# Late query features from a quarter of the array's rows per head, and reciprocals spread by a product with ones

## The chip, the cores and the metric

One core of a Trainium2 chip runs a whole decoder layer in one launch. The metric is the device time in microseconds (us). The kernel before took 2324.54 us, the median of three runs (2317.61 to 2330.41).

The engines of the core have the names of the profile: PE is the matrix engine (PEld its loading of the stationary operand), DVE, ACT and POOL are the vector, scalar and GpSimd engines, SP is the engine from whose queue most DMAs are issued. SBUF is the working memory with 128 partitions, PSUM the memory that PE writes, in banks of 128 x 512 fp32.

## The reference

A pre-norm decoder layer on x of 2 x 2048 tokens by 512: `x + attn(ln(x))`, then cross attention on a context of 154 tokens, then a mixture of experts. Only the first part is touched, a linear attention with 16 heads of 32 dimensions and 128 features:

```python
q_proj = _elu1(jnp.einsum('bhnd,hdf->bhnf', q, proj_matrix))
k_proj = _elu1(jnp.einsum('bhnd,hdf->bhnf', k, proj_matrix))
kv = jnp.einsum('bhnf,bhnd->bhfd', k_proj, v)
attn = jnp.einsum('bhnf,bhfd->bhnd', q_proj, kv)
k_sum = k_proj.sum(axis=2)
z = 1.0 / (jnp.einsum('bhnf,bhf->bhn', q_proj, k_sum) + 1e-08)
attn = attn * z[..., None]
out = attn.transpose(0, 2, 1, 3).reshape(b, n, d)
return out @ w_out + b_out
```

`_elu1(x)` is x + 1 for x > 0 and exp(x) otherwise. All is fp32.

## The kernel before

**Blocks and chunks.** The 4096 tokens are 8 blocks of 512 (`TB`), 4 to each batch (`bpb`). Everything is held with features in the partitions and tokens in the free dimension. A chunk is a pair (block b, c) with c from 0 to 3: 128 of the 512 dimensions, that is 4 heads of 32.

**Products in parts.** Where fp32 accuracy is wanted from the `fp32r` format, an operand is kept as a high part (an ACT copy) and a low part (`low`, line 116: source minus high part), and a product is three terms, high x high, low x high and high x low (`TERMS`, line 142; `product`, line 144).

**Queries and keys for the features.** A head has only 32 rows. `to_heads` (line 356) stores a chunk's projection, high and low, in DRAM (`qd`). `stack` (line 292) loads it back as 96 rows: high, low, high, in three DMAs. The projection matrix lies as 96 rows too (`pst`: high, high, low), so that one product of 96 rows gives the sum of all three terms. `query_features` (line 476) makes one such product for one head, into one of the 4 PSUM banks of the pool `sc`, and `features` (line 361) makes `_elu1` of it: two ACT passes and one DVE instruction.

**Sums.** `numerators` (line 485) multiplies the four heads' features with `kv`, each head in its own quarter of the array's columns; `denominators` (line 507) does the same with the key sums into a bank `pd` that is held for the block's four chunks. `columns.matmul` (line 229) keeps these in program order.

**Reciprocals.** `reciprocals` (line 522) adds the epsilon, stores the 16 x 512 denominators in DRAM (`dd`), loads them as 128 x 64 (`turned`), takes the reciprocal on DVE and stores it (`stored`, `zd`). `load_reciprocals` (line 548) loads them for two chunks, each head's row broadcast to that head's 32 partitions, in four DMAs into a tile `zr`.

**Attention's end.** `attended` (line 558) multiplies numerators by `zr` on POOL, copies to the high part on ACT and takes the low part on DVE. `attention_out` (line 567) multiplies by `w_out` and adds x and the bias (`out_tile`, line 304). For the first batch the numerators lie in DRAM meanwhile (`numd`), and `load_numerators` (line 544) fetches 1 MB for a block through POOL's queue.

**Order.** `Dense` (line 175) holds a list of generators of large products; `dense.fill(n)` issues n of them, and `dense.after(n, do)` does something n products later. Three loops matter:

- The key loop (line 1306) goes over all 8 blocks, with the first batch's queries made during the second batch's keys, one head at a time. At its item (7, 3, 0) it loads what the next stage wants first (line 1320).
- A short loop (line 1334) ends those queries.
- The late loop (line 1346) makes the second batch's queries, 16 chunks in 17 steps. A step issues two heads' features, 13 products of `dense` (14 from step 12), a quarter of an attended block, and the same again; then the sums of the chunk before. `ahead` (line 1345) says which block's halves are attended in which step. Queries are loaded a step ahead, reciprocals likewise.

Behind the late loop the cross attention begins (line 1390); the last block is attended in its first steps.

**Buffers.** `big` has 17 buffers of 8 KB per partition (`eight`), `work` the tiles of `half` (9) and of `pair_of` (4), `ps` and `sc` four PSUM banks each. A framework places the waits and orders the instructions of each engine, except where program order is kept.

Of the kernel before, what the change touches and what calls it, by code (L numbers as in the profile page):

```python
# [17 lines left out]
P = 128  # L18
# [12 lines left out]
Z_EPS = 1e-8  # L31
LAG = 3
SC = 4
GROUP = 2


@with_exitstack
def decoder_layer(
# [65 lines left out]
    def pair_of(name, n=TB):  # L104
        return work.tile([P, 2, n], FR, tag="hl", name=name, bufs=4)
# [14 lines left out]
    def load_weight(w, name):  # L120
        raw = eight([P, NC, w.shape[1]], F32, f"raw_{name}")
        for k in range(NC):
            nc.sync.dma_start(out=raw[:, k], in_=w[k * P : (k + 1) * P, :])
        return [raw[:, k] for k in range(NC)]

    def split_weight(raw, name, busy=False):

        hi = eight([P, NC, D], FR, f"{name}_hi")
        lo = eight([P, NC, D], FR, f"{name}_lo")
        for k in range(NC):  # L130
            if isinstance(raw, list):
# [216 lines left out]
    rest = slice(2 * HD, 3 * HD)  # L348
    low(pst[rest], praw[rest], pst[rest])
    wq = split_weight(load_weight(w_qkv[:, :D], "wq"), "wq")  # L350

    kvs, kszs, pkvs, kaccs, made_kv = [], [], [], [], []
    qd = [[dram.tile([2, P, TB], F32, name=f"qd{b}_{c}") for c in range(NC)] for b in range(nblk)]
# [7 lines left out]
    def features(src, name, e=None):  # L361

        e = half(f"e_{name}") if e is None else e
        nc.scalar.activation(e, src, AF.Relu, scale=-1.0)  # L364
        nc.scalar.activation(e, e, AF.Exp, scale=-1.0)  # L365
        nc.vector.scalar_tensor_tensor(e, src, 0.0, e, ALU.max, ALU.add)  # L366
        return e
# [102 lines left out]
    qsts, qps, pds, nums, numd, zrs, zds, ats = {}, {}, {}, {}, {}, {}, {}, {}  # L470

    def load_queries(b, c):
        qsts[b, c] = eight([3 * HD, 4, TB], FR, f"qst{b}_{c}")
# [2 lines left out]
    def query_features(b, c, h):  # L476
        head = slice((4 * c + h) * FEAT, (4 * c + h + 1) * FEAT)
        pp = sc.tile([P, TB], F32, tag="sc", name=f"pqp{b}_{c}_{h}")
        nc.tensor.matmul(pp, lhsT=pst[:, head], rhs=qsts[b, c][:, h, :], start=True, stop=True)
        e = None  # L480
        if b < bpb and h:
            e = early.tile([P, TB], F32, tag="eq", name=f"eq{b}_{c}_{h}")
        qps[b, c, h] = features(pp, f"q{b}_{c}_{h}", e)

    def numerators(b, c):
        if c == 0:
# [35 lines left out]
    def reciprocals(b, pd):  # L522

        den = half(f"den{b}")
        nc.vector.tensor_scalar(den, pd, Z_EPS, None, ALU.add)
        dd = dram.tile([4, NC, TB], F32, name=f"dd{b}")
        for h in range(4):
            nc.sync.dma_start(out=dd[h], in_=den[h * HD : h * HD + NC, :])
        z = small.tile([P, H * TB // P], F32, tag="z", name=f"z{b}", bufs=1)
        flat = "h c n -> (h c n)"  # L530
        zd = dram.tile([4, NC, TB], F32, name=f"zd{b}")

        def turned():
            nc.sync.dma_start(out=z, in_=dd.rearrange(flat).rearrange("(p n) -> p n", p=P))

        def stored():
            tc.keep_in_program_order(nc.vector.reciprocal(z, z))
            nc.sync.dma_start(out=zd.rearrange(flat).rearrange("(p n) -> p n", p=P), in_=z)

        dense.after(10, turned)  # L540
        dense.after(26 if b < nblk - 1 else 24, stored)
        zds[b] = zd
# [2 lines left out]
        nums[b] = eight([P, NC, TB], F32, f"num{b}")  # L545
        nc.gpsimd.dma_start(out=nums[b], in_=numd[b])

    def load_reciprocals(b, c):
        two = pair_of(f"zr{b}_{c}").bitcast(F32)
        for h in range(4):  # L550
            nc.sync.dma_start(
                out=two[h * HD : (h + 1) * HD],
                in_=zds[b][h : h + 1, c : c + 2].to_broadcast([HD, 2, TB]),
            )
        for i in range(2):
            zrs[b, c + i] = two[:, i]

    def attended(b, c):

        if c == 0:  # L560
            ats[b] = [eight([P, NC, TB], FR, f"at{b}_{i}") for i in range(2)]
        at = nums[b][:, c]
        nc.gpsimd.tensor_tensor(at, at, zrs.pop((b, c)), ALU.mult)
        nc.scalar.copy(ats[b][0][:, c], at)
        low(ats[b][1][:, c], at, ats[b][0][:, c])

    def attention_out(b, t):
        if not 0 <= b < nblk:
# [737 lines left out]
    for n in range(nblk * per):  # L1306
        b, c, t = n // per, n // NT % NC, n % NT
        dense.fill(58 if n == 0 else fl(n, 9.25) if n < 32 else fl(n, 9.5))
        if (b, c, t) == (nblk - 1, 0, 0):
            context_load()  # L1310
        if (b, c, t) == (nblk - 1, 1, 0):
            xwk = split_weight(wk_t, "xwk")
            dense.add(*(context_key(i, xwk) for i in range(NC)))
        if (b, c, t) == (nblk - 1, 2, 0):
            xwv = split_weight(wv_t, "xwv")
            bvr = half("bvr")
            nc.sync.dma_start(out=bvr, in_=bv.to_broadcast([P, D]))
# [24 lines left out]
    wout = split_weight(w_out, "wout")  # L1342
    steps = chunks[bpb * NC :]

    ahead = {n if n < 13 else n + 2: ((n - 1) // 2, (n - 1) % 2 * 2) for n in range(1, 15)}
# [44 lines left out]
    for n in range(len(steps) + LAG + 1):  # L1390
        if n < len(steps):
# [4 lines left out]
            if b == 0:  # L1396
                if k == 0:
                    load_values(0)
                if k in (NC - 1 + 0, NC + 1 + 0):
                    load_reciprocals(nblk - 1, k - 0 - NC + 1)  # L1400
# [222 lines left out]
```

## Time and profile before

| | |
|---|---|
| three runs, us | 2317.61, 2324.54, 2330.41 |
| profiled execution, us | 2323.77 |
| its span, first to last instruction, us | 2321.7 |
| mean granted clock of PE | 0.988 |
| PE busy | 2234.2 us (96%) |
| DVE, POOL, ACT busy | 1675.2, 1225.3, 1101.6 us |
| DMA moved | 498.23 MB, mean 215 GB/s |
| query feature products (line 479) | 128, from 232.3 to 635.1 us |
| multiplies by the reciprocals (line 563) | 32, from 480.6 to 677.3 us |

The profile comes from one execution. An engine's busy time is the time in which it had an instruction under way; a PE product's end is modelled, and products overlap, so their distance from start to start says more than their duration. The granted clock is the share of full speed that PE's throttle let through. Idle time of an engine is put down to what released it. A wait for a DMA is counted until its data had landed. Where an engine's own time is near the whole span, as PE's is, the other engines matter by what PE waits for.

### The profile page before, as it was taken

Reading aid. Unit: us, or ns where it says so; the run is one execution under the profiler, and the core shown is the slowest. Engines: PE = TensorE matmul, PEld = TensorE weight load, DVE = VectorE, ACT = ScalarE, POOL = GpSimd, SP = SyncE. Lnnn points to the kernel's source line nnn. Section 1 sums busy time; section 2 is a strip of 40 time slices with the busy share of each in tenths; the row PEclk is TensorE's granted clock in tenths of the full one; section 3 lists DMA queues with packets and bytes.
Section 4 is the critical chain, followed back from the end, with each engine's and each line's share of the span. In section 5 each row is a group of like instructions: output and inputs, shape, how many; then the busy total and the mean of one; then the engine's idle time right before and its main releaser. Section 6 shows DMA issues by size and latency. Waiting matters only on the chain.

```text
span 2321.7 us, 35182 instructions
## 1 busy us (share of the span) xinstructions
PE 2234.2 (96%) x11978; PEld 1733.5 (75%) x11978; DVE 1675.2 (72%) x2733; ACT 1101.6 (47%) x2598; POOL 1225.3 (53%) x1078
## 2 busy tenths in 40 slices
PE   7999999898989999999999999999999999999999
PEld 5888777645667777766787877888878888788887
DVE  6554555568587777878877776788787887877777
ACT  4555677656466676765343343222433223432221
POOL 5555333446475565554766454555474554755443
PEclk9999999989999999999999999999999999999999
DMA  7656777889975665666867557665547666575553
GB/s 213 182 169 176 201 219 215 248 235 278 249 216 153 171 183 170 183 183 223 287 237 260 216 185 292 226 232 226 195 168 281 231 231 235 196 281 204 209 190 132
DMA packets 201809, 498.23 MB, mean 215 GB/s; under 512 B 27738, under 2 KB 47578, under 8 KB 181694
## 3 DMA queue, kind: packets, MB, share of 16 engines
q1 hardware_dynamic: 199902, 489.89, 64.2%
q0 software_dynamic: 1728, 6.09, 0.9%
q8 instruction: 96, 1.57, 0.3%
q14 instruction: 83, 0.68, 0.1%
HBM read 351.30 MB, written 144.60 MB: 214 GB/s over the span
## 4 chain that ended last, share of the span: by engine, by line
PE 73%; DMA 12%; DVE 6%; issue 3%; ACT 2%; POOL 2%; SPq 1%; DVEq 0%; ACTq 0%; POOLq 0%
PE pg L1082 30%; PE pf L1195 11%; PE pf L148 4%; PE pk L148 3%; PE pv L148 3%; PE pq L148 3%; PE po_x L148 3%; PE xpq L148 2%; PE pp L402 2%; PE pc L745 1%; PE pkv L230 1%; PE psc L693 1%; DMA qst<-qd 1%; PE xpt L725 1%; ACT xe L703 1%
## 5 line engine op out<-in xcount | busy, mean ns | idle before, releaser
L1082 PE MATMUL pg<-xo,wq 128*128 128x512 f32 x3360 | 823.2, 393 | 3.4 <-DVE xo L118 1.4
L1082 PEld LDWEIGHTS pg<-xo,wq 128*128 128x128 f32 x3360 | 630.4, 188 | 143.0 <-DVE xo L118 3.4
L407 POOL TENSOR_TENSOR kacc<-kacc,e_k 128x512 f32<-128x512 f32 x128 | 166.0, 1297 | 225.4 <-DVE e_k L366 206.3
L1216 DVE TENSOR_TENSOR sum<-sum,pf 128x512 f32<-128x512 f32 x376 | 251.2, 683 | 45.9 <-PE pf L1195 41.3
L703 ACT ACTIVATE xe<-psc,nb 128x154 f32<-128x154 f32 x512 | 195.2, 417 | 87.5 <-DVE nb L700 81.7
L708 POOL TENSOR_TENSOR xe<-xe,sm 128x616 f32<-128x616 f32 x128 | 157.7, 1237 | 93.6 <-DVE sm L707 61.3
L1195 PE MATMUL pf<-ht,wdo 128*128 128x512 f32 x696 | 185.5, 393 | 4.9 <-DVE sum L1216 3.2
L1145 POOL TENSOR_TENSOR u<-u,gr 128x512 f32<-128x512 f32 x48 | 65.1, 1356 | 227.3 <-DVE u L1114 226.6
L366 DVE SCALAR_TENSOR_TENSOR e_k<-pp,e_k 128x512 f32<-128x512 f32 x128 | 87.4, 684 | 108.5 <-ACT e_k L365 102.4
L1113 ACT ACTIVATE u<-u 128x512 f32<-128x512 f32 x80 | 50.6, 633 | 231.6 <-DVE u L1102 231.5
L1195 PEld LDWEIGHTS pf<-ht,wdo 128*128 128x128 f32 x696 | 130.8, 188 | 35.7 <-issue 3.3
L1195 PE MATMUL pf<-hb,wdo 128*128 128x512 f32 x522 | 146.8, 398 | 1.0 <-DVE sum L1216 0.9
L148 PE MATMUL pf<-wd,hp 128*128 128x512 f32 x528 | 135.1, 403 | 5.4 <-DVE mv_n L248 3.4
L148 PEld LDWEIGHTS pf<-wd,hp 128*128 128x128 f32 x528 | 100.2, 192 | 34.6 <-issue 6.5
L700 DVE TENSOR_REDUCE nb<-psc 128x2 f32<-128x308 f32 x256 | 111.3, 464 | 12.0 <-PE psc L693 11.8
L703 ACT ACTIVATION_READ_ACCUMULATOR xe<-psc,nb 128x1 f32 x512 | 118.3, 231 | 0.0
L1102 DVE TENSOR_TENSOR u<-u,pg 128x512 f32<-128x512 f32 x160 | 107.9, 680 | 13.5 <-PE pg L1082 12.5
L1195 PEld LDWEIGHTS pf<-hb,wdo 128*128 128x128 f32 x522 | 97.2, 188 | 24.8 <-DVE sum L1216 3.6
L364 ACT ACTIVATE e_k<-pp 128x512 f32<-128x512 f32 x128 | 76.8, 601 | 69.5 <-PE pp L402 62.5
L693 PE MATMUL psc<-xkst,xst 96*128 96x154 f32 x512 | 91.8, 286 | 11.7 <-ACT xe L703 10.8
L693 PEld LDWEIGHTS psc<-xkst,xst 96*128 96x128 f32 x512 | 77.7, 193 | 27.1 <-ACT xe L703 18.0
L402 PEld LDWEIGHTS pp<-pst,kst 96*128 96x128 f32 x512 | 76.1, 192 | 27.8 <-issue 5.8
(285 smaller groups left out, 5118.7 us busy)
## 6 DMA issues: line engine op xcount, KB each, us to landing
wq<-wqs SPq DMA_DIRECT2D x90, 1024.0 KB
wqs<-wq SPq DMA_DIRECT2D x30, 1024.0 KB
wdo<-wds SPq DMA_DIRECT2D x29, 1024.0 KB
kst<-kd SPq DMA_DIRECT2D x96, 256.0 KB
qst<-qd SPq DMA_DIRECT2D x96, 256.0 KB
xst<-xqd SPq DMA_DIRECT2D x96, 256.0 KB
wdo<-wds SPq DMA_DIRECT2D x29, 768.0 KB
kd<-khl SPq DMA_DIRECT2D x32, 512.0 KB
```

Of the source, the lines that this page charges most:

```text
L148: nc.tensor.matmul(dst, lhsT=a, rhs=b, start=n == 0, stop=n == len(todo) - 1)
L366: nc.vector.scalar_tensor_tensor(e, src, 0.0, e, ALU.max, ALU.add)
L402: nc.tensor.matmul(pp[:, h], lhsT=stks[b, c][:, h, rows], rhs=pst[:, head], start=True, stop=True)
L407: nc.gpsimd.tensor_tensor(acc, acc, kp, ALU.add)
L693: nc.tensor.matmul(psc[:, i], lhsT=xsts[b, c][:, h, t * P : (t + 1) * P], rhs=ksts[bt, c][:, h, :], start=True, stop=True,)
L700: nc.vector.tensor_reduce(nb[:, two], psc, AX.X, ALU.max, negate=True)
L703: nc.scalar.activation(e[:, h, :], psc[:, i], AF.Exp, bias=nb[:, h : h + 1], accum_out=sm[:, h : h + 1],)
L708: nc.gpsimd.tensor_tensor(e, e, sm.unsqueeze(2).to_broadcast([P, 4, keys]), ALU.mult)
L1082: nc.tensor.matmul(pb, lhsT=w[:, p, i, k, :], rhs=xop[:, q, k, :], start=first and m == 0, stop=m == len(todo) - 1, skip_group_check=True,)
L1102: nc.vector.tensor_tensor(dst, dst, pb, ALU.add)
L1195: nc.tensor.matmul(banks[i], lhsT=w[:, p, i * P : (i + 1) * P], rhs=t[q], start=new and m == 0, stop=m == len(TERMS) - 1, skip_group_check ...
L1216: nc.vector.tensor_tensor(dst, dst, banks[i], ALU.add)
```

## The change

The early queries (first batch) stay as they are. For the second batch's queries:

- **Loads.** A chunk's high and low parts are loaded as they lie in DRAM, 128 rows with a head in each quarter of 32, no longer in three stacked copies. `load_pair` loads two chunks into one buffer, one DMA each, about three steps ahead. The projection matrix comes once more, as 128 rows with a head in each quarter, and is split (`load_rows`).
- **Features.** `chunk_features` makes all four heads of a chunk at once: three terms, each with four products of 32 rows, one in each quarter of the array's rows, into four banks, kept in program order. In step n it stands straight behind the sums of chunk n - 1 and makes the features of chunk n + 1.
- **Reciprocals.** They are split into high and low parts and stored as 32 rows (16 high, 16 low). `load_reciprocals` loads a block's 32 rows in one DMA. `spread_setup` makes a matrix of zeros and ones, and `attended` lets PE multiply the rows by it, so that each head's reciprocal stands in its 32 rows of a PSUM bank `pz`. DVE multiplies the numerators by the bank; the low part goes from DVE to POOL.
- **Order.** The first two blocks' reciprocals and numerators are loaded at item (7, 3, 0), later numerators a block earlier than before; block 5 is attended one step later.

The diff, cut to its core:

```diff
+    prows = []
+    def load_rows():
+        raw = half("prow").rearrange("p (c f) -> p c f", c=NC)
+        for h in range(4):
+            nc.sync.dma_start(
+                out=raw[h * HD : (h + 1) * HD],
+                in_=proj.rearrange("d (c h f) -> d h c f", c=NC, h=4)[:, h],
+            )
+        pair = eight([P, 2, NC, FEAT], FR, "prows")
+        nc.scalar.copy(pair[:, 0], raw)
+        low(pair[:, 1], raw, pair[:, 0], nc.gpsimd)
+        prows.append(pair)
...
+    def load_pair(b, c):
+        two = eight([P, 2, 2, TB], FR, f"qh{b}_{c}")
+        for i in range(2):
+            qsts[b, c + i] = two[:, i]
+            nc.sync.dma_start(
+                out=two[:, i].bitcast(F32), in_=qd[b][c + i].rearrange("r p n -> p r n")
+            )
...
+    def chunk_features(b, c):
+        pps = [sc.tile([P, TB], F32, tag="sc", name=f"pqp{b}_{c}_{h}") for h in range(4)]
+        for n, (i, j) in enumerate(TERMS):
+            for h in (3, 2, 1, 0):
+                rows = slice(h * HD, (h + 1) * HD)
+                columns.matmul(
+                    pps[h],
+                    lhsT=prows[0][rows, i, c, :],
+                    rhs=qsts[b, c][rows, j, :],
+                    start=n == 0,
+                    stop=n == 2,
+                    skip_group_check=True,
+                )
+        for h in range(4):
+            qps[b, c, h] = features(pps[h], f"q{b}_{c}_{h}")
...
         def stored():
             tc.keep_in_program_order(nc.vector.reciprocal(z, z))
-            nc.sync.dma_start(out=zd.rearrange(flat).rearrange("(p n) -> p n", p=P), in_=z)
+            nc.scalar.copy(zhl[:, 0], z)
+            low(zhl[:, 1], z, zhl[:, 0])
+            nc.sync.dma_start(
+                out=zd.rearrange("r h c n -> r (h c n)").rearrange("r (p n) -> p r n", p=P),
+                in_=zhl.bitcast(F32),
+            )
...
-    def load_reciprocals(b, c):
-        two = pair_of(f"zr{b}_{c}").bitcast(F32)
-        for h in range(4):
-            nc.sync.dma_start(
-                out=two[h * HD : (h + 1) * HD],
-                in_=zds[b][h : h + 1, c : c + 2].to_broadcast([HD, 2, TB]),
-            )
-        for i in range(2):
-            zrs[b, c + i] = two[:, i]
+    def spread_setup():
+        both = eight([P, 1 + SPREAD, TB], FR, "spread")
+        nc.gpsimd.memset(both.bitcast(F32), 0.0)
...
+        nc.vector.tensor_tensor(to, *rows, ALU.add)
+        spread.append(both)
+
+    def load_reciprocals(b):
+        nc.sync.dma_start(
+            out=spread[0][: 2 * H, 1 + b % SPREAD].bitcast(F32),
+            in_=zds[b].rearrange("r h c n -> (r h c) n"),
+        )
...
     def attended(b, c):
...
+        pz = bank(f"pz{b}_{c}")
+        nc.tensor.matmul(
+            pz,
+            lhsT=spread[0][:, 0, c * P : (c + 1) * P],
+            rhs=spread[0][:, 1 + b % SPREAD],
+            start=True,
+            stop=True,
+        )
         at = nums[b][:, c]
-        nc.gpsimd.tensor_tensor(at, at, zrs.pop((b, c)), ALU.mult)
+        nc.vector.tensor_tensor(at, at, pz, ALU.mult)
         nc.scalar.copy(ats[b][0][:, c], at)
-        low(ats[b][1][:, c], at, ats[b][0][:, c])
+        low(ats[b][1][:, c], at, ats[b][0][:, c], nc.gpsimd)
...
         if (b, c, t) == (nblk - 1, 3, 0):
+            load_rows()
             load_numerators(0)
-            load_reciprocals(0, 0)
+            load_numerators(1)
+            spread_setup()
+            load_reciprocals(0)
+            load_reciprocals(1)
             bout = load_row(b_out, "bout")
...
-        if m % 4 == 1:
-            load_queries(*chunks[bpb * NC])
+        if m % 4 == 2 and m < (nblk - bpb) * per:
+            load_pair(bpb, 0)
+        if m % 4 == 3 and m >= (nblk - bpb) * per:
+            load_pair(bpb, 2)
+            chunk_features(bpb, 0)
...
-            if n + 1 < len(steps):
-                load_queries(*steps[n + 1])
-        if n + 1 in ahead:
-            load_reciprocals(*ahead[n + 1])
+            if n % 2 and n + 3 < len(steps):
+                load_pair(*steps[n + 3])
+        if n + 1 in ahead and not ahead[n + 1][1] and ahead[n + 1][0] > 1:
+            load_reciprocals(ahead[n + 1][0])
...
         for i in range(2):
-            if n < len(steps):
-                query_features(b, c, 2 * i)
-                query_features(b, c, 2 * i + 1)
             dense.fill(fl(2 * n + i, 13 if n < 12 else 14))
             if n in ahead:
                 attended(ahead[n][0], ahead[n][1] + i)
...
-                    if whole + 1 < bpb:
-                        load_numerators(whole + 1)
-            if n and i:
+                    if whole + 2 < bpb:
+                        load_numerators(whole + 2)
+            if i and n:
                 columns.batch()
                 numerators(*steps[n - 1])
                 denominators(*steps[n - 1])
+            if i and n + 1 < len(steps):
+                chunk_features(*steps[n + 1])
```

In the cross attention's first steps the last block's reciprocals are likewise loaded once instead of twice.

More of the change, by code (lines that the diff above doesn't have):

```diff
@@ L33 @@
 SC = 4
+SPREAD = 3
 GROUP = 2
@@ L468, in decoder_layer @@
         dense.add(*tr[2:3], query_chunk(b, 1), *tr[3:], query_chunk(b, 2), query_chunk(b, 3))
-    qsts, qps, pds, nums, numd, zrs, zds, ats = {}, {}, {}, {}, {}, {}, {}, {}
+    qsts, qps, pds, nums, numd, zds, ats = {}, {}, {}, {}, {}, {}, {}
+    def load_pair(b, c):
[5 more added lines that the diff above has]
+            )
     def load_queries(b, c):
@@ L528, in reciprocals @@
             nc.sync.dma_start(out=dd[h], in_=den[h * HD : h * HD + NC, :])
-        z = small.tile([P, H * TB // P], F32, tag="z", name=f"z{b}", bufs=1)
+        zhl = small.tile([P, 2, H * TB // P], FR, tag="z", name=f"z{b}", bufs=1)
+        z = zhl[:, 1].bitcast(F32)
         flat = "h c n -> (h c n)"
-        zd = dram.tile([4, NC, TB], F32, name=f"zd{b}")
+        zd = dram.tile([2, 4, NC, TB], F32, name=f"zd{b}")
         def turned():
@@ L546, in load_numerators @@
         nc.gpsimd.dma_start(out=nums[b], in_=numd[b])
-    def load_reciprocals(b, c):
-        two = pair_of(f"zr{b}_{c}").bitcast(F32)
-        for h in range(4):
-            nc.sync.dma_start(
-                out=two[h * HD : (h + 1) * HD],
-                in_=zds[b][h : h + 1, c : c + 2].to_broadcast([HD, 2, TB]),
-            )
-        for i in range(2):
-            zrs[b, c + i] = two[:, i]
+    spread = []
+    def spread_setup():
+        both = eight([P, 1 + SPREAD, TB], FR, "spread")
+        nc.gpsimd.memset(both.bitcast(F32), 0.0)
+        rows = [
+            ident[: 2 * H, r * H : (r + 1) * H]
+            .rearrange("p (h c) -> p c h", h=4)
+            .unsqueeze(3)
+            .to_broadcast([2 * H, NC, 4, HD])
+            for r in range(2)
+        ]
+        to = both[: 2 * H, 0].rearrange("p (c h d) -> p c h d", c=NC, h=4)
+        nc.vector.tensor_tensor(to, *rows, ALU.add)
[5 more added lines that the diff above has]
+        )
     def attended(b, c):
@@ L1338, in decoder_layer @@
             sums_step(m)
-        if m % 4 == 1:
-            load_queries(*chunks[bpb * NC])
+        if m % 4 == 2 and m < (nblk - bpb) * per:
[3 more added lines that the diff above has]
+            chunk_features(bpb, 0)
     wout = split_weight(w_out, "wout")
     steps = chunks[bpb * NC :]
-    ahead = {n if n < 13 else n + 2: ((n - 1) // 2, (n - 1) % 2 * 2) for n in range(1, 15)}
+    ahead = {n if n < 11 else n + 1 if n < 13 else n + 2: ((n - 1) // 2, (n - 1) % 2 * 2) for n in range(1, 15)}
     for n in range(len(steps) + 1):
@@ L1398, in decoder_layer @@
                     load_values(0)
-                if k in (NC - 1 + 0, NC + 1 + 0):
-                    load_reciprocals(nblk - 1, k - 0 - NC + 1)
+                if k == NC - 1:
+                    load_reciprocals(nblk - 1)
                 if NC + 0 <= k < 2 * NC + 0:
```

## The prediction

> **What bounds it now.** TensorE (PE) is busy 96% of the span, so a change pays only where PE idles or runs at a lowered clock. I read the forty slices first (the PE row is 9 nearly throughout and dips at slices 7 and 8, where the DMA row stands at 9), then the table of stretches, then who waited for whom, the DMA issues and the timeline of PE. These are the stretches of 20 us from the end of the key loop to the first cross scores; the columns are the stretch, its length, PE busy, weight loads, VectorE (DVE), ScalarE (ACT), GpSimd (POOL), the granted clock, the busy share of the 16 DMA engines, GB/s.
>
> ```profile
> 440.00:460.00 20.00, 15.18 (x113) 10.90 (x102) 8.46 (x12) 8.84 (x18) 9.32 (x8) 0.91 0.97 297
> 460.00:480.00 20.00, 16.62 (x133) 10.63 (x132) 13.60 (x22) 14.89 (x30) 7.36 (x7) 0.83 0.99 282
> 480.00:500.00 20.00, 17.99 (x89) 7.54 (x88) 12.37 (x22) 7.63 (x15) 10.08 (x9) 0.91 0.76 220
> 500.00:520.00 20.00, 19.16 (x95) 10.30 (x96) 13.41 (x20) 13.41 (x27) 9.50 (x9) 0.91 0.92 230
> 520.00:540.00 20.00, 17.00 (x85) 10.12 (x83) 14.70 (x22) 11.47 (x21) 10.31 (x8) 0.97 0.95 278
> 540.00:560.00 20.00, 18.85 (x93) 12.82 (x93) 17.25 (x31) 12.01 (x23) 14.18 (x17) 0.95 1.01 289
> 560.00:580.00 20.00, 18.13 (x102) 10.72 (x95) 18.96 (x27) 15.67 (x30) 15.96 (x12) 1.00 0.90 267
> 580.00:600.00 20.00, 18.19 (x90) 12.75 (x94) 11.07 (x18) 9.06 (x18) 9.98 (x9) 1.00 0.96 255
> 600.00:620.00 20.00, 19.36 (x106) 11.30 (x94) 14.75 (x24) 12.36 (x23) 14.50 (x19) 1.00 0.79 211
> 620.00:640.00 20.00, 18.07 (x93) 12.48 (x93) 9.18 (x15) 9.02 (x17) 2.53 (x2) 1.00 1.04 283
> 640.00:660.00 20.00, 12.98 (x76) 8.86 (x69) 16.13 (x36) 10.93 (x46) 10.51 (x13) 0.87 0.68 176
> ```
>
> Here the DMA engines are full (0.9 to 1.04) and PE is not. As full-clock time of PE I take busy times clock; what a row lacks to 20 us is lost. A, 440 to 480: 6.2+6.2 = 12.4 us. B, 480 to 640 (the late queries): 3.6+2.6+3.5+2.1+1.9+1.8+0.6+1.9 = 18.0. C, 640 to 660: 8.7. Together 39.1 us. The three rows before (380 to 440) lose 1.4 us of 60, or 2.3%, by the same sum; the two behind (660 to 700) lose 0.8 of 40. So 39 us is nearly all that this change can win here.
>
> Why PE loses it: waits from 440 to 660, all engines (waiter, releaser, us in total, times, longest), then PE's alone.
>
> ```profile
> ACT at L564 <- POOL num L563: 33.2, 15, 6.7
> POOL num L563 <- DMA zr<-zd: 27.7, 4, 17.0
> POOL xr_a L312 <- DMA xr_a<-in_x: 24.1, 8, 7.2
> DVE at L118 <- ACT at L564: 22.9, 6, 7.7
> ```
>
> ```profile
> PE pqp L479 <- DVE e_q L366: 8.1, 6, 2.8
> PE psc L693 <- ACT xe L703: 5.5, 2, 3.1
> PE pqp L479 <- DVE eq L366: 5.0, 2, 3.9
> PE pqp L479 <- DMA qst<-qd: 1.9, 1, 1.9
> ```
>
> POOL waits for the broadcast reciprocals (zr, 27.7 us) or the numerators (num, 17.6 us), ACT for POOL, DVE for ACT; DVE takes its work in order, so the feature sums e_q stand behind that one `low`, and PE waits for the PSUM bank that e_q frees. At 588 DVE stands 7.7 us so, at 528 5.2 us. What fills the DMA engines (430 to 660; issues, KB each):
>
> ```profile
> qst<-qd SPq DMA_DIRECT2D x54, 256.0 KB
> zr<-zd SPq DMA_DIRECT2D x60, 128.0 KB
> ```
>
> **Removed traffic.** Late queries: 16 chunks by 3 copies of 256 KB = 12.6 MB in 48 issues become 16 issues of 512 KB = 8.4 MB. Reciprocals: 17 loads (the first is made twice) of four 128 KB = 8.9 MB in 68 issues become 8 of 64 KB = 0.5 MB. Added: 0.25 MB of projection rows in 4 issues and 32 KB more in each store of z. Net 12.3 MB of the 55.7 MB that 253 GB/s moved from 440 to 660: the share of 0.91 would fall to 0.71. On SP's queue 116 issues become 28, at the median 0.41 to 0.43 us of a row some 37 us of its time.
>
> **The stall's chain.** `attended` no longer begins on POOL: PE spreads the reciprocals into a bank, DVE multiplies from it, ACT copies, POOL takes `low`. On DVE the 1.13 us of at (x28 here) goes and a multiply with a PSUM operand comes, at 0.68 (the row xr_a<-xr_a,po_a): 28 x 0.45 = 13 us less. On POOL 1.43 (num) goes and 1.41 (`low` of ht) comes: nothing. The numerators of block 1 load with those of block 0, and each later one a block earlier: one row loads in 9.3 to 11.5 us, a block's turn comes every two steps, some 18, so the 17.6 us wait goes and DVE's multiply is not held. What is late next is xr_a from DRAM (24.1 us on POOL, in the same crowded queues, so shorter), and behind it PE itself.
>
> What I take back: B to the rate of the rows before, 160 x 2.3% = 3.7 us, a gain of 14.3 (it could be 4 if POOL's xr_a waits hold PE instead). A is mixed: at 444 PE waits 3.9 us for eq, which is an early query and stays; the weights of 1 MB stay; 1.5 MB of zr goes, 1 MB of num comes in. A third of it, 4.4 (0 to 6). C: the scores wait for an ACT and a DVE that stand behind layer-norm loads issued late on SP: about half, 4 (0 to 7). Sum: 22.7 (4 to 27).
>
> **What PE gets to do.** From the timeline (start, busy, form):
>
> ```profile
> 545.99 1.06 PE L230 MATMUL pn<-e_q,kv 128*32 128x512 f32 x8
> 546.87 1.04 PE L230 MATMUL pd<-e_q,ksz 128*32 128x512 f32 x8
> 547.84 0.50 PE L479 MATMUL pqp<-qst,pst 96*128 96x512 f32 x1
> ```
>
> A dense product starts every 0.23 us (po_a from 548.17 on). Spread: 32 products of that form, 7.4 us, all on the path. Features: 4 products of 96 rows, two of which take 0.47 (550.92 to 551.39), so 0.94 a chunk, become 12 of 32 rows, in three rounds of four. The trace has no quarter of rows. The nearest row is the quarter of columns: pn's eight are two passes of four heads, and the second pass starts 0.43 us after the first (431.04, 431.47 in an earlier chunk), the four of a pass within 0.01 us, side by side; so a round of products that take 0.23 alone could take 0.23. Twelve weight loads instead of four bound it otherwise: four key products of 128 columns (pp at 429.81) step every 0.10, so 0.40 a round. One after the other would be 0.92. I take 0.31, midway between the two nearer rows: 0.93, plus 0.09 for the second change of shape (pd's eight hold PE 0.97, pn's 0.88): 1.02. Per chunk +0.08, by 16: 1.3 us (from 16 x (0.69-0.94) = -4.0 to 16 x (2.85-0.94) = +30.6).
>
> The Trainium skill speaks against this at two places. "TensorEngine Tiling (Array Packing)", Key Properties, says that a change of tiling mode drains the array; the 0.09 above agrees in kind, and one change more per chunk makes 1.4 us. "TensorE: Matmul & The Clock Gate", LDWEIGHTS, says that a load's time goes by its columns, not its rows; the trace agrees (192 ns for 96 rows, 188 for 128), so splitting rows triples the loading. Its Part 3 gives 3.07x for four row tiles of 512 columns, which no run here shows; by that the chunk would take 12 x 0.23 / 3.07 = 0.90, and the sum would be 2 us lower.
>
> Small, and covered while DVE, ACT and POOL have a third of the stage free: the memset of spread (POOL, 1.89 us by kacc's row of the same size), the splits of the projection rows and of z (ACT 0.62 and POOL 1.4 once; for z at most the reciprocal's 0.54 each, twice, eight times, on a chain with about a step of 9 us to spare). Without that cover they would be some 12 us. Features are now made a step further ahead of their sums, so the late e_q no longer stands between dense products.
>
> **Sum** on the profiled execution: span 2321.7, outside it 2.1, its time 2323.8 (0.8 under the median). 2323.8 - 22.7 + 7.4 + 1.3 = 2309.8, so 2310. My forecast's own range is 2299 to 2318.
>
> **Rivals.**
> 1. The stall moves to PE. Reciprocals are now an operand of PE, which takes products in order: a `spread` that lands late, which cost POOL 17 us once and PE nothing directly, stops PE. pz also takes one of four banks of ps, one of which pd holds for four steps, and three more tiles (rows, spread, numerators) want buffers of big near 450. For: zd of block 6 was issued at 622.4 and its reader released at 628.2, behind full queues. Against: the queues are emptier, and the load has a step of lead. Half of the 22.7 returned: 2321.
> 2. The other side, slower: row quarters do not run side by side. Price 30.6 instead of 1.3: 2309.8 + 29.3 = 2339. It decides from about 0.6 us a round (three rounds then cost 1.8+0.1, 16 times 0.96 more = 15.4, which eats the gain), and it is past 0.5% near 0.85.
> 3. More than I take: A and C fall nearly to the quiet rate too (7 of the 39 us left): 2323.8 - 32 + 8.7 = 2300.
>
> **Numbers.** Forecast 0.56, rival 1 0.18, rival 2 0.16, rival 3 0.10. About 0.5% (11.6 us) can be told from no change: faster is below 2312.9, slower above 2336.2. Faster: 0.42 of the forecast's 0.56 and rival 3, 0.52. Same: 0.14 of the forecast, 0.15 of rival 1, 0.01 of rival 2, 0.30. Slower: 0.03 of rival 1, 0.15 of rival 2, 0.18. The range takes in the forecast, rivals 1 and 3 and the low end of 2: 2295 to 2330.
>
> **What would show it.** Right: DMA share near 0.7 from 480 to 640, no DVE at waiting on ACT for us at a time, the twelve feature products of a chunk starting within 1 us, PE waits on e_q gone. Wrong: feature products 0.23 us apart, PE waiting for DMA spread or for num's multiply, PE busy below 18 of 20 in this stage with DMA engines idle.

## The result, and the profile after

The changed kernel takes 2358.39 us (median of 4 runs, 2352.05 to 2362.8) where the kernel before took 2321.97 on the same chip (4 runs): a ratio of 1.0149, 95% interval 1.0129 to 1.017. It is some 35 us slower; 2310, 13.8 us faster, was forecast, in a range up to 2330. Ratios, here and below, leave out slow executions: two of the ten of e13, at 3377 and 6344 us. The profiled execution spans 2355.7 us, 34.0 more than that of before.

**The same stretches after** (stretch, length, PE busy, weight loads, DVE, ACT, POOL, granted clock, DMA share, GB/s):

```profile
480.00:500.00 20.00, 15.73 (x81) 6.80 (x85) 9.55 (x17) 2.52 (x5) 5.26 (x5) 0.66 0.64 225
500.00:520.00 20.00, 16.42 (x96) 5.52 (x88) 11.92 (x20) 13.06 (x26) 9.41 (x9) 0.86 0.52 183
520.00:540.00 20.00, 20.00 (x100) 11.33 (x92) 11.78 (x21) 7.31 (x15) 6.46 (x7) 0.97 0.62 220
540.00:560.00 20.00, 20.00 (x113) 11.92 (x116) 16.22 (x30) 10.60 (x21) 11.87 (x14) 1.00 0.52 174
560.00:580.00 20.00, 19.68 (x116) 12.18 (x115) 11.82 (x20) 12.23 (x24) 12.04 (x10) 1.00 0.42 143
580.00:600.00 20.00, 19.35 (x102) 11.55 (x103) 14.09 (x24) 12.89 (x26) 10.40 (x9) 1.00 0.53 177
600.00:620.00 20.00, 18.82 (x100) 10.38 (x99) 10.58 (x16) 9.12 (x18) 10.95 (x9) 1.00 0.51 176
620.00:640.00 20.00, 19.00 (x106) 11.18 (x105) 10.96 (x21) 8.23 (x17) 11.26 (x17) 1.00 0.58 170
640.00:660.00 20.00, 16.11 (x77) 10.13 (x76) 6.44 (x11) 9.33 (x19) 1.30 (x1) 1.00 0.76 204
660.00:680.00 20.00, 14.13 (x61) 7.82 (x65) 15.44 (x28) 7.42 (x17) 8.66 (x11) 0.70 0.25 79
```

From 480 to 640 the DMA share fell from 0.92 (mean of eight rows) to 0.54, and from 440 to 660 from 0.91 to 0.63, where 0.71 was forecast: the relief is there, more than forecast. By the prediction's sum (20 less busy times clock) the stretch loses 19.2 us where it lost 18.0. From 520 to 640 it loses 3.8 where it lost 11.8, so PE is full there, but not with the old work: much of what fills it is new. And 640 to 680 lose 14.0, where they lost 9.5.

**Who waits, 440 to 660, all engines** (waiter, releaser, us in total, times, longest):

```profile
POOL xr_a L313 <- DMA xr_a<-in_x: 38.4, 11, 12.5
ACT at L633 <- DVE num L632: 32.2, 12, 7.1
ACT e_q L379 <- PE pqp L231: 25.1, 8, 8.6
POOL at L119 <- ACT at L633: 23.1, 10, 7.8
```

The zr and num loads are gone from the list, as predicted. But POOL waits longer for xr_a, 38.4 us for 24.1, with the DMA engines half idle; and ACT, which stood behind POOL, stands behind PE and DVE. PE's own waits from 430 to 720:

```profile
PE pqp L231 <- DVE e_q L381: 8.6, 5, 5.2
PE pqp L503 <- DVE eq L381: 5.3, 1, 5.3
PE psc L762 <- DVE e_q L381: 4.2, 2, 3.7
```

The waits on e_q did not go: they were 8.1 us at the feature products.

**The new products.** First a chunk whose twelve run in one piece, then one that is cut up (start, busy, form). Starts tell what a product costs the stream.

```profile
567.36 0.39 PE L149 MATMUL po_a<-wout_lo,at 128*128 128x512 f32 x1
567.68 0.97 PE L231 MATMUL pqp<-qh,prows 32*128 32x512 f32 x12
568.58 0.72 PE L149 MATMUL po_a<-wout_hi,at 128*128 128x512 f32 x2
```

```profile
524.76 0.50 PE L231 MATMUL pqp<-qh,prows 32*128 32x512 f32 x1
525.19 0.50 PE L624 MATMUL pz<-spread 128*128 128x512 f32 x1
525.52 0.63 PE L149 MATMUL po_a<-wout_hi,at 128*128 128x512 f32 x2
526.09 0.50 PE L231 MATMUL pqp<-qh,prows 32*128 32x512 f32 x2
526.51 0.50 PE L149 MATMUL po_a<-wout_lo,at 128*128 128x512 f32 x1
526.85 0.40 PE L149 MATMUL po_a<-wout_hi,at 128*128 128x512 f32 x1
527.18 0.97 PE L231 MATMUL pqp<-qh,prows 32*128 32x512 f32 x9
528.08 0.50 PE L149 MATMUL po_a<-wout_hi,at 128*128 128x512 f32 x1
```

Row quarters do run side by side: twelve products hold PE from 567.68 to 568.58, 0.90 us, where 0.23 each, one after the other, would be 2.8. In the second chunk the framework's order of PE's stream has 1, then 2, then 9 of them, with dense products between; presumably it puts each where it expects the bank to be free. The three pieces hold PE 0.43 + 0.42 + 0.90 = 1.75 us, and the first full-size product behind each takes 0.33 instead of 0.23 (525.19 to 525.52), 0.1 each more. The 16 chunks came in 38 pieces; 5 chunks came whole.

**Where the 34.0 us went** (the trace cut at three places: the first product of the second context value, the last `pd`, the first output product of the cross attention's second block). Up to the first cut +6.3, the late stage +29.0 (158.5 to 187.5), the first cross attention -2.3, the rest +1.0. In the late stage, by what each product holds PE until the next starts, and with the half-clock stretches taken out: features 18.0 to 26.2 (+8.2), spread +9.2, first dense products after a change of shape +2.9, all together +20.7. Half-clock stretches (the granted clock is 0.5 in them), most of which follow idle time, hold 18.7 us of products where they held 6.7: +6.0, half the difference. Idle time: +2.7, from 13.8 to 16.5. (The three come to 0.4 more than the 29.0: so rough is the split.)

### The profile page after: what moved, and what is told of

Read it like the earlier page. It is cut to its first block, busy times and chain, and to the rows that moved or that the text cites. A ratio compares the mean times of both kernels' runs of the same rounds, so it can differ in the third digit from the quotient of the medians.

```text
span 2355.7 us, 35365 instructions
## 1 busy us (share of the span) xinstructions
PE 2266.2 (96%) x12138; PEld 1744.3 (74%) x12138; DVE 1669.8 (71%) x2742; ACT 1100.8 (47%) x2607; POOL 1219.5 (52%) x1080
## 4 chain that ended last, share of the span: by engine, by line
PE 53%; DMA 5%; DVE 5%; ACT 2%; issue 2%; POOL 1%; SPq 1%; ACTq 0%; DVEq 0%; POOLq 0%
PE pg L1151 29%; PE pf L1264 11%; PE pf L149 4%; PE po_x L149 3%; PE xpq L149 2%; PE pc L814 1%; PE psc L762 1%; PE xpt L794 1%; ACT xe L772 1%; DMA wds<-wdq 1%; DMA xqd<-xhl 1%; DMA xsx<-x 1%; DMA x<-xr_x 1%; DMA wq<-wqs 1%; DVE wq L119 1%
## 5 line engine op out<-in xcount | busy, mean ns | idle before, releaser
L769 DVE TENSOR_REDUCE nb<-psc 128x2 f32<-128x308 f32 x256 | 111.1, 465 | 14.9 <-PE psc L762 14.8
L762 PEld LDWEIGHTS psc<-xkst,xst 96*128 96x128 f32 x512 | 78.8, 196 | 25.5 <-ACT xe L772 14.3
```

Of the source, the lines that this page charges most:

```text
L762: nc.tensor.matmul(psc[:, i], lhsT=xsts[b, c][:, h, t * P : (t + 1) * P], rhs=ksts[bt, c][:, h, :], start=True, stop=True,)
L769: nc.vector.tensor_reduce(nb[:, two], psc, AX.X, ALU.max, negate=True)
```

## The experiments

Three theories stood at first for the price: S (the cut runs), P (the spread products on PE) and W (DVE's wait for layer-norm loads, 7.9 us near 656). After e1 to e4 came B: a chunk now wants all four `sc` banks at once, so it waits until ACT and DVE have evicted the whole chunk before, while the old form went round the banks one at a time. Ratios are against the kernel before on the same chip, with 95% intervals.

Where the runs differ from the kernel before, by the same three cuts (us, from one profiled execution each; that of e1 took 2376.21, 13 above its median):

| run | up to the late stage | late stage | first cross attention | rest |
|---|---|---|---|---|
| changed kernel | +6.3 | +29.0 | -2.3 | +1.0 |
| e1, features alone | +0.8 | +43.2 | +1.3 | +7.5 |
| e12, features, two heads at a time | -0.7 | +26.7 | -4.5 | +1.6 |
| e2, spread alone | -5.5 | +4.9 | +8.3 | +7.3 |
| e14, e2 with doubled products | +1.4 | +4.7 | +8.0 | +2.8 |
| e11, e2 without products | +12.2 | -1.8 | +15.3 | 0.0 |
| e16, change without products | +8.9 | +40.7 | -5.5 | +4.8 |
| e7, change, short eviction | +1.5 | +14.1 | 0.0 | +2.9 |
| e8, before, short eviction | -2.5 | -7.9 | +15.3 | +2.9 |
| e10, before, fewer loads | -0.6 | -7.0 | +6.3 | +6.5 |
| e13_again, before, fewer still | -0.8 | -6.6 | -1.1 | +2.5 |

e8, e10 and e11 gain in the late stage and lose more elsewhere. So some 10 us of a total can come from how the rest falls into place, and the late stage tells more of an edit than the whole.

**One part alone.**

```diff
 (e1: kernel before + load_rows, load_pair, chunk_features; broadcast zr kept)
 (e2: kernel before + reciprocals, spread_setup, attended and order of the change; stacked queries kept)
```

> The kernel before with the late features from row quarters alone (queries loaded as they lie, twelve products a chunk); reciprocals still broadcast by DMA and multiplied on POOL. Theory S (the twelve products are cut up: the profile of the change shows 38 runs instead of 16, a lone one holding PE 0.45 us, a whole run 0.89): about +8 to +12 us on the kernel before, 2330 to 2334. Theory P (the spread products on PE are what costs): no more than +3. Theory W (the late wait of DVE for layer-norm loads is what costs): +3 or less, as the multiply is not on DVE here.

> The kernel before with the spread reciprocals alone (and their earlier loads and numerators); late features from 96 stacked rows as before. Theory P: 32 products at 0.23 to 0.33 us add 7 to 11 us on PE, and with the lighter DMA traffic (8.4 MB less) some of that comes back: +2 to +10, 2324 to 2332. Theory S: at or below the kernel before, since nothing is cut up: 2310 to 2322. Theory W: +10 or more, with a stall of 5 us near 660 behind a layer-norm load.

e1: 2363.07, 1.0152 (1.0129 to 1.0176). e2: 2337.08, 1.0049 (1.0031 to 1.0067). The features alone cost as much as the whole change, the spread about 11 us, most of it behind the late stage; together more than the change, so they don't add. None of the first theories had put e1 above 2334. Two of PE's waits in e1 (430 to 720) name the place:

```profile
PE pqp L230 <- DVE e_q L381: 18.4, 6, 7.0
PE po_a L148 <- DVE num L546: 5.2, 2, 3.3
```

**Whole runs.** e3 makes the four banks one tile, e6 keeps them apart and lets a chunk's first product wait for the four DVE instructions that end the chunk before.

```diff
 (e3)
-        pps = [sc.tile([P, TB], F32, ...) for h in range(4)]
+        four = sc.tile([P, 4, TB], F32, ...)
+        pps = [four[:, h] for h in range(4)]
 (e6)
+                if n == 0 and h == 3:
+                    for done in ended[-4:]:
+                        tc.add_manual_dep(ins.ins, done.ins.name, ...)
```

> The whole change, with the four PSUM banks of a chunk's features taken as one tile, so that the twelve products stand together (16 runs instead of 38). Theory S: 22 runs fewer at 0.45 plus about 0.1 for the way back to dense products, 10 to 12 us less than the change: 2346 to 2348. Theories P and W: within 4 us of the change, 2354 to 2362.

> The whole change, with the first of a chunk's twelve products made to wait for the DVE instructions that end the chunk before's features, so that no dense product stands within a run (16 runs, four separate banks as in the change). Theory S (the cuts cost): 22 runs fewer, 10 to 12 us less than the change, 2346 to 2348. Theory B (a chunk needs all four banks of sc at once, so a run can't start before the last head of the chunk before is evicted; cut runs were only the form that this wait took): the wait stands in one piece before each run instead, 2353 to 2368.

e3: 2385.02, 1.0248 (1.022 to 1.0275); one tile also made the heads' evictions follow each other, so it overstates. e6: 2358.59, 1.0137 (1.0116 to 1.0158), the changed kernel's time, with 16 whole runs. The products' hold on PE in the stage fell from 26.8 to 15.5 us, and idle time rose from 16.5 to 31.0. So S falls as the price: what whole runs saved on PE came back as idle time. PE's first waits in e6:

```profile
PE pz L637 <- DVE num L559: 8.4, 2, 7.7
PE pqp L231 <- DVE e_q L384: 5.9, 2, 4.5
```

The longest, 7.7 us, is a pz product that wants a bank of `ps` that DVE has yet to empty; so not all of the idle time stands at the new products.

**The eviction shortened.** The exponential, with its two ACT passes, is left out of the late queries' features, which leaves one DVE instruction a head (other values); e8 is the same on the kernel before.

```diff
-            qps[b, c, h] = features(pps[h], f"q{b}_{c}_{h}")
+            e = qps[b, c, h] = half(f"e_q{b}_{c}_{h}")
+            nc.vector.tensor_scalar(e, pps[h], 0.0, 1.0, ALU.max, ALU.add)
```

> The whole change, with the late features shortened to one DVE instruction straight from the bank (the exponential is left out, two ACT passes a head go). Theory B: a bank is free some 2 us after its product instead of 5 to 7, runs stand whole (19 by the program's order) and PE no longer waits for them: 25 to 35 us less than the change, 2323 to 2333. Theory S: the 10 us of the cuts alone, about 2348. Theory P (spread): no change beyond S.

> The kernel before with the same shortening of the late features (the exponential is left out). Control for the run above. Theory B: one bank a head, taken in a ring, hides the eviction already, so 0 to 8 us less, 2314 to 2326. If this falls by 20 us or more as well, eviction bounds both kernels and theory B says nothing of the change.

e7: 2339.14, 1.0054 (1.0033 to 1.0076), 19 us below the changed kernel, though above the 2333 that B allowed. e8: 2335.79, 1.0044 (1.0029 to 1.006), no gain at all, but a loss of some 10 us, outside the range too. In the late stage the shorter eviction saves the changed kernel 14.9 us and the one before 7.9, which that one loses again in the cross attention. So eviction weighs on both, and about twice as much on the changed kernel.

**Two banks at a time.** e9 is the changed kernel with two heads behind the sums and two half a step later; e12 is that form of the features alone on the kernel before.

```diff
+            if not i and n < len(steps):
+                chunk_features(b, c, (2, 3))
...
-                chunk_features(*steps[n + 1])
+                chunk_features(*steps[n + 1], (0, 1))
```

> The changed kernel (2358.4), but a chunk's row quarters are made two heads at a time: six products into two banks behind the sums, six into the other two after the half step's dense products. Each run then needs only two of the four banks of sc, and the two before it are evicted meanwhile, as in the kernel before. PE's own work hardly changes: three rounds of 0.23 plus a change of shape, 0.8 a run, 32 runs, 25 us against the 26 that the products hold in the changed kernel. Theory B (a run that needs all four banks waits for the whole eviction of the chunk before) expects most of the 19 us that shortening the eviction gave: 2340 to 2348. The rival, that changes of shape and small products cost PE by themselves, expects 2355 to 2362.

> The kernel before with the row quarters two heads at a time and nothing else of the change: the broadcast reciprocals stay. With all four heads at once this alone took 2363. Theory B expects 2330 to 2340, since the rest of the price is PE's extra 7 us (25 held against 18); the rival expects 2355 or more. Under 2320 would mean that the smaller loads of queries pay after all.

e12: 2344.8, 1.0071 (1.0049 to 1.0092): half of e1's price is gone, though it too misses its range, 2330 to 2340. e9: 2351.28, 1.0105 (1.009 to 1.0121): better than the change's 1.0149, but it misses the 2340 to 2348. Of e9's waits on e_q at the new products 2.7 us are left, and the products hold PE some 29 us at full clock (33 pieces, 0.88 each) against 18 before: six products in two quarters hold PE as long as twelve in four. In e12 they hold it 30 us, but PE still waits on e_q (430 to 720), at the new products and at the first scores:

```profile
PE pqp L230 <- DVE e_q L381: 7.6, 3, 4.2
PE psc L734 <- DVE e_q L381: 6.3, 1, 6.3
```

B is right for about half of the features' price. The rest is in part what the new products hold PE; how much is not shown.

**Layer norm.** Block 1's statistics are pinned in DVE's order, so that DVE doesn't stand behind them.

```diff
-            made[t] = normalize(load_tile(d, at, t, ...), ...)
+            made[t] = normalize(load_tile(d, at, t, ...), ..., pinned=name == "x" and b == 1)
```

> The whole change, with the statistics of block 1's layer norm held on DVE behind everything that the program lists before them, so that no late feature sum stands behind a layer-norm load. Theory W: the two waits of PE of 5.2 and 3.7 us near 656 and 671 go, and with them a stretch of half clock: 8 to 12 us less than the change, 2346 to 2350. Theories S and P: within 4 us of the change.

2366.13, 1.0163 (1.0137 to 1.0188). The late stage fell from 187.5 to 179.1, the first cross attention rose from 122.0 to 137.6. What is gained near 656 is lost later; W falls.

**Less traffic, no new work.** e10 is the kernel before with the reciprocals loaded once, e13 also with the stacked late queries of two chunks for all.

```diff
 (e10, in load_reciprocals)
+        if kept:
+            for i in range(2):
+                zrs[b, c + i] = kept[0][:, i]
+            return
 (e13, also in load_queries, late blocks)
+            if c in once:
+                qsts[b, c] = once[c]
+                return
```

> The kernel before with the broadcast reciprocals loaded once and used for all chunks (the reciprocals of the other chunks are left out): 8.4 MB and 64 DMA issues less, no work added on any engine. The premise of the prediction (full DMA queues cost PE most of 39 us): 12 us or more below the kernel before, 2300 to 2313. Rival: PE's waits come from the order in which DVE and POOL take their work, and from single loads' latency, not from the bytes: within 5 us of the kernel before.

> The kernel before with its own PE work, but the reciprocals are loaded once and the late queries' stacked rows for two chunks alone, and all later chunks use these (other values; 19.4 MB and 106 issues of loads are left out, more than the 12.3 MB net of the change). If full DMA queues cost PE most of the 39 us that the prediction counted, the time falls to 2295 to 2310, and the change paid its own PE work out of that gain. If the traffic costs PE nothing at the end, as 8.4 MB less suggested (2331.9 measured), 2320 to 2334.

> The same kernel as e13_light, once more, because the execution that was profiled there took 6342 us and shows nothing of the others (2318.9 median). If the gain in the late stage is as large as the prediction's 18 us and is given back behind it, the late queries and the part up to the last scores are shorter by that and the cross attention longer; if the stage itself gains little, PE idles there for something else than loads.

e10: 2331.85, 1.0017 (1.0003 to 1.0031): no gain from 8.4 MB. e13: 2318.89, 0.9967 (0.9947 to 0.9987); again, 2319.42, 0.997 (0.9949 to 0.9991). So 19.4 MB less, without any work added, bring about 7 us. The late stage is some 7 us shorter in both; e10 loses that behind it. (Both keep the tiles that they use again in buffers of `big` for good, and POOL's multiply no longer waits for a load each time; what that does alone was not tried.) Four of the stretches of e13_again:

```profile
500.00:520.00 20.00, 19.30 (x104) 11.56 (x105) 16.26 (x24) 13.53 (x26) 15.01 (x13) 1.00 0.53 182
520.00:540.00 20.00, 19.46 (x103) 12.34 (x105) 18.68 (x32) 13.35 (x25) 18.11 (x18) 1.00 0.56 179
540.00:560.00 20.00, 16.69 (x82) 10.59 (x74) 15.55 (x20) 10.57 (x20) 14.36 (x11) 0.94 0.45 138
580.00:600.00 20.00, 18.07 (x86) 11.61 (x85) 15.41 (x19) 7.27 (x14) 13.90 (x12) 0.91 0.37 129
```

The DMA share is 0.53 from 480 to 640, and the loss 16.2 us, by the same sum as the 18.0 of before. At 540 the DMA engines are half idle and PE loses 4.3. The queue from which the loads are issued suggests why; SP's longest waits from 440 to 700, before, after, and in e13_again:

```profile
SPq L316 <- DVE xr_a L315: 18.9, 11, 6.5
```

```profile
SPq L317 <- DVE xr_a L316: 60.7, 20, 10.9
```

```profile
SPq L316 <- DVE xr_a L315: 45.0, 19, 8.3
```

In the changed kernel SP stands from 571.2 to 575.5 at the store of a finished tile, which waits for DVE's last addition, and from 575.9 to 577.5 at the next; the loads of xr_a that come behind them are issued from 577.9 on. We read it so: with fewer loads in it, the queue runs up to the stores and stands there, and the loads behind are issued that much later. A full queue had become a waiting one.

**What makes the spread dear.** e5 and e15 are two parts of its order alone on the kernel before (numerators a block earlier; block 5 a step later). e14 is e2 with every product with ones made twice. e11 is e2, and e16 the changed kernel, with the product left out and the numerators multiplied by themselves.

```diff
 (e11, e16)
-        pz = bank(f"pz{b}_{c}")
-        nc.tensor.matmul(pz, lhsT=spread[0][:, 0, c * P : (c + 1) * P], ...)
...
-        nc.vector.tensor_tensor(at, at, pz, ALU.mult)
+        nc.vector.tensor_tensor(at, at, at, ALU.mult)
```

> The kernel before with the numerators of the first batch loaded a block earlier and nothing else. The prediction said that POOL's longest wait for them, 17.6 us, goes. If that wait held PE, 2 to 5 us less, 2321 to 2324. If the full queues or the end take it back, 2326 as before; if the earlier loads push others late, up to 2332.

> The kernel before with one part of the change's order alone: block 5 is attended one step later. No work is added or removed. If the moved order is what made the spread reciprocals dear beyond their products, 2332 to 2340. If it costs nothing, 2320 to 2330.

> The kernel before with the spread reciprocals alone (2337.1 measured), each product with ones made twice into the same bank; nothing else moves. If PE is the bound there and each product costs what it holds PE (0.30 us, 32 of them), 9 to 10 us more: 2345 to 2348. If such products fall into idle time, 2335 to 2340.

> The kernel before with the spread reciprocals alone (2337.1 measured), but the product with ones and its bank are left out: DVE multiplies the numerators by themselves, so the attention has other values. Splits, stores, loads, the DVE multiply and the moved order stay. If the product on PE, its bank and its wait are the price (theory P), the time falls to 2326 to 2330. If it is the chain behind (DVE's multiply in its order, the moved loads and splits), it stays at 2334 to 2340.

> The changed kernel (2358.4) without the product with ones: DVE multiplies the numerators by themselves (other values), everything else stays. If the product's time on PE (9.2 us in the stage) is its price, 2346 to 2351. If the spread's price lies in the chain behind it, 2355 to 2362. The same edit on the spread reciprocals alone went the other way (2349.8 against 2337.1), with its losses outside the late stage.

e5: 2327.79, 1.0016 (1.0 to 1.0032). e15: 2326.81, 1.0008 (0.9994 to 1.0022). e14: 2340.03, 1.0056 (1.0036 to 1.0075), hardly above e2's 1.0049, though the products hold PE 14.3 us in the stage for 8.3. Six us more on PE show as 0.07%, 1.6 us; by the intervals alone a price of PE time one to one isn't excluded. But the late stage stays as long as e2's, and PE's idle time in it falls from 13.2 to 7.9: there the second products went into idle time, and P is not borne out.

Most of e2's price lies behind the stage, where PE waits (640 to 720) 4.6 us for POOL's `xe` and 2.4 for the load of `spread`; what brings that about is open.

e11: 2349.76, 1.0096 (1.0081 to 1.0112), and e16: 2372.21, 1.0202 (1.0182 to 1.0222), both some 12 us *slower* without the product, and above both ranges. The groups of DVE's multiply, changed kernel and e16 (430 to 720; count, busy, mean ns):

```profile
L632 DVE TENSOR_TENSOR num<-num,pz 128x512 f32<-128x512 f32 x32 | 21.5, 677 | 6.8 <-PE pz L624 6.6
```

```profile
L624 DVE TENSOR_TENSOR num<-num 128x512 f32<-128x512 f32 x32 | 31.7, 1018 | 0.4
```

The mean is 1018 ns instead of 677, 10.2 us more of DVE time, but a mean misleads here: in e16 19 of the 32 take 0.67 to 0.69 us, as with the bank, and the other 13 take 0.72 to 3.47, each of them while POOL has an instruction under way (e11: 17 and 15). In the changed kernel none takes above 0.69, with POOL at work or not. The edit also moved the multiplies, which no longer wait for the reciprocals: the first comes at 479.6 instead of 506.4. PE's waits on e_q at the new products rose from 8.6 to 16.8 us. In e11 the late stage even became 6.7 us shorter than e2's; the loss stands ahead of it and behind. So the edit changes DVE's time and its order along with the product, and says nothing clear on the product.

## Why the prediction was wrong, step by step

The time measured lies some 48 us above the sum. Two terms failed: the features' 1.3 us, which alone cost 35 (e1) and so decide that the kernel became slower, and the 22.7 us taken back, of which the runs show about 7.

- **The first step that failed: "What I take back", 22.7 us.** The rows were read rightly in the main (PE not full, DMA engines full, though three of the eleven rows are below 0.8), the cause was not. Taking the traffic away without adding work gave about 7 us (e13), or nothing (e10); in the late stage it gave 7 in both, where 14.3 was taken. As we read them, the waits in the list were links of a cycle DVE, SP's queue, loads, POOL, ACT, DVE, and removing one link let the others wait instead. "xr_a ... in the same crowded queues, so shorter" came out as 24.1 to 38.4 us.
- **Removed traffic**: right in bytes (12.1 MB less in the whole kernel, for 12.3), and the share fell further than the 0.71 forecast (0.63 from 440 to 660). For the most part it wasn't what PE waited for.
- **The second, and larger: features, 1.3 us (bounds -4.0 to +30.6).** The disputed size was nearly right: 0.90 a run, where 0.93 was taken, so rival 2 (not side by side) is out. The Trainium skill's "TensorE: Matmul & The Clock Gate", Part 3, gave 0.90 by its 3.07x, and that is what the trace shows. Two things were missing. A run was costed as one piece, and it came in pieces, +8.2 us on PE and part of the +2.9 behind. And the banks were not asked for at all: four at once, with no bank left to fill while DVE empties. The prediction made e_q early for the sums, but the wait that PE had on it stood at the next feature products before, and stood there after. Alone these features cost 35 us, above even the upper bound (e1); half of it goes with two banks at a time (e12); the other half is only in part explained.
- **Before's chunk, 0.94**, was read from one pair of products; over the stage a product of 96 rows holds PE 0.295, 1.18 a chunk. This error was in the change's favour.
- **A change of shape, 0.09 a chunk**: a full product behind one takes 0.10 more, which agrees in kind with the same skill's "TensorEngine Tiling (Array Packing)", Key Properties. A lone row-quarter product holds PE 0.43, where a full product takes 0.23, which was not costed.
- **Spread, 7.4 us**: 9.2 on PE in the stage (0.33 each, not 0.23). The part alone costs some 11 us. Its price is not shown to be the products: 6 us more of them added 1.6, inside the uncertainty, and nothing to the late stage. Its two moves of order cost 4 and 2 us, neither clearly apart from nothing. Most of it lies behind the late stage, and its cause stays open.
- **The stall's chain**: the multiply at 0.68 on DVE was right (0.677), and the numerators' and reciprocals' waits went. The wait of `at` on ACT went from DVE, with its `low`, to POOL (23.1 us). PE waiting for spread is 1.3 us once, so rival 1 did not decide (2.4 in e2 behind 640, 4.7 in e14 from 480 to 720).
- **C, 4 us**: 640 to 680 got worse: DVE waits up to 7.9 us for a layer-norm load there; e4 shows that mending it there is paid later.
- **The signs named**: of those for right, the share fell and no DVE `at` waits (POOL has that work now); twelve products within 1 us came for 5 of 16 chunks; "PE waits on e_q gone" failed. Of those for wrong one came: PE is busy 15.7 and 16.4 of 20 from 480 to 520, with DMA shares of 0.64 and 0.52.

Shown: that the features carry the price (e1), that half of it goes when a run asks for two banks instead of four (e12), that whole runs alone win nothing (e6), that a shorter eviction shortens the changed kernel's late stage about twice as much as that of the kernel before (e7, e8), the pieces on PE (trace), the small worth of the traffic (e10, e13). Argued only: that the half-clock stretches (+6.0 us) are the price of the idle ones ahead of them, and that SP's order is what turns freed queues into waits; no run changed that order. Open: the other half of the features' price. Giving the new form more than four banks, which would test B directly, was not tried.

## What to carry to other kernels

Before packing products side by side, count the banks that the pack wants at once, and ask what is left to write into while they are emptied; a product that shares the array can undo a ring of banks. A full DMA row beside an idle PE isn't a cause until a run without the loads, and with as little else changed as can be, is faster. And a run that takes work out can come out slower (e8, e10, e11): cut the trace into parts, and see whether the difference lies where the edit is, before you call it the price of what was edited.

## What was not expected of the hardware

- A DVE multiply of 128 x 512 fp32 with one operand in PSUM took 0.63 to 0.69 us, whether POOL worked beside it or not (changed kernel). With both operands from SBUF 19 of 32 took 0.67 to 0.69, and 13 took 0.72 to 3.47, all of these with POOL at work (e16; 17 and 15, up to 1.79, in e11).
- Twelve products of 32 rows in four row quarters in one run held PE 0.89 to 0.91 us, some 0.075 each; six in two row quarters as long (e9); one alone 0.43; the full-size one behind 0.33.
- The granted clock fell to half in stretches of 3.4 us and its multiples: 18.7 us of PE's products in the late stage ran so after the change, 6.7 before, 38.8 in e1's profiled execution.
